# Two attention layers over 8 images: row 0 copied, bias rows, 264 columns, and other places for the steps of the sums

## Chip, cores and metric

The kernel runs on one core of a Trainium2 chip. The metric is the device time of one execution in microseconds (us), here the median of several runs; lower is better. An engine is written as in the profile: PE is TensorE's matmul, PEld its weight load, DVE VectorE, ACT ScalarE, POOL GpSimd, SP SyncE, which here only issues DMAs. "L857" is line 857 of the kernel before.

## What is computed

Eight images of 256 channels and 96x96 pixels in float32 go through two layers, each with a group norm ahead of it and the input added after it. Cut to what matters:

```python
# layer 0, on g = groupnorm(x)
q_f, k_f, v_f = (fft2(pconv(g, w, b), axes=(-2, -1)) for w, b in ((w1, b1), (w2, b2), (w3, b3)))
q_f, k_f = l2_normalize(q_f), l2_normalize(k_f)        # shape (b, 8 heads, 32, 9216)
attn = einsum('bhcn,bhdn->bhcd', q_f, k_f) * temperature
attn = complex(softmax(real(attn)), softmax(imag(attn)))
out = abs(ifft2(einsum('bhcd,bhdn->bhcn', attn, v_f), axes=(-2, -1)))   # over 32 and 9216
x = x + pconv(out, w_out)
# layer 1, on g = groupnorm(x)
q, k = softplus(Wq g + bq), softplus(Wk g + bk)        # 32 rows each
v = Wv g + bv
x = x + einsum(q, k v^T) / einsum(q, sum(k))
```

The forward transform is over the two axes of the image and the inverse one over the flattened 9216 pixels, so the two don't cancel: in the kernel each image row is turned by an amount that grows with the number of its row. Row 0 isn't turned at all.

## The kernel before

No transform is carried out. Layer 0's logits come from two 256x256 sums over pixels (`pair_sums`, L317), of the even part (x plus its mirror image) and of the odd part (x minus it). Everything is worked per image, and the stages of one image follow each other on PE: attention, woven into the turning of the rows (`attention` L364, `rotate` L524); `images` (L576, the 2-D maps, magnitude, output projection); `layer1` (L674); `output` (L829). Two arenas hold 256x9216 floats each and change roles from image to image: `x_of(b)` and `y_of(b)`.

**Weaving.** A stage is a generator that yields numbers. `weave` (L878) adds them up, and each time a whole one is due it takes one step of another generator. During attention the other is `rotate(b)`, one step for two rows. During images, layer1 and output the other is `pair_sums(b + 1)`, the sums of the next image: a step is four 128x128 transposes of 128 columns (tile `eoT`, L344), an ACT copy to `xT` (L347), and four products into the accumulators `acc` (L325), with its `bn_stats` on DVE (L259). The sums have 37 steps; those left over are taken in one go at the end (`finish`, L887). The last image has no next one. Whoever yields more in one place takes a step more there, and leaves one fewer for a later place. A part that is left under one at the end of a stage is dropped.

**Order.** In attention the order of PE is as written (L897), in output that of PE, DVE, POOL and SP (L903). Elsewhere a scheduler orders the instructions. PE, DVE, ACT, POOL and SP each run their own queue in order.

**Rotation.** `step` (L535) takes two rows at once: four transposes of 128x96 (`xr`, L546), an ACT copy (L557), and two steps later four products with a 96x97 window of the table `rt` (`y`, L549; each float32 product is two PE instructions, a transpose is one). DVE takes 96 of the 97 columns to `y_of(b)` as image column g, in reverse order (L554), and the last one to `ys` (L553). The window comes from DRAM by DMA (L531), its last column from `csn` on POOL (L532), which is zero for row 0.

**Attention.** `qkm` (L389) holds four rows of means of q and k; L394 adds the biases to them by four products of a column `b12col` with the identity; ACT copies them (L400). At the end L510 forms `mz` from the columns of `at`: 33 x 8 = 264 that are used and 24 that stay zero, which fill the 288 up to two blocks of 128 and one of 32; DVE scales them (L512).

**Denominators.** At the end of `layer1`, DVE copies `kx` (L796); PE transposes it (L799, L801); DVE makes `kse4` of it (L807); PE forms eight products `den` (L816) and two `am` (L822); DVE takes the reciprocal `rec` of `den` (L819). `output` spreads `rec` over the partitions by PE (L833) and multiplies `kq` by it on DVE (L838). The yields between are 0.5 (L797), 0.5 (L810), 1 (L825), and 1 after the first four normalizations (L850).

**Output.** For each of six `s` and two halves `m` there is a group of four products `o` of 32x128 by 32x384 (L857), one in each block of 32 rows of PE. Three of the four results are added to x by DVE (L862); the fourth is copied by ACT (L865) and added by POOL (L866). Each group ends with `yield 1` (L871). The transposes, `rec` and `o` all take their PSUM tiles from one pool of five (`psum`, L53), which are handed out in turn:

```python
    psum = ctx.enter_context(tc.tile_pool(name="psum", bufs=5, space=bass.MemoryType.PSUM))
                for j in range(NB):
                    ps = ps_tile(f"o_{b}_{s}_{m}_{j}")
```

**Start.** All 25 loads of image 0 stand first on SP. `tables` (L226) builds the lookup tables, among them `rt` by a DMA on SP (L249) that waits for DVE, and `load_small` (L198) puts 51 small loads behind it. It is called after the first step of the sums of image 0 (L892). The tables' inputs lie in the arena `y_of(0)` (L134).

Of the kernel before, what the change touches and what calls it, by code (L numbers as in the profile page):

```python
# [68 lines left out]
def two_layer_kernel(ctx: ExitStack, tc: tile.TileContext, x, w1t, b1, w2t, b2, w3, b3, wot, temp,  # L69
# [56 lines left out]
    def ps_tile(name):  # L126
        return psum.tile([P, 512], F32, tag="ps", name=name)

    def load_x(b, t):
        for c in (2 * (NT - 1 - t), 2 * (NT - 1 - t) + 1):  # L130
            for h, n in chunk_rows(c):
                nc.sync.dma_start(out=x_of(b)[:, :, x_col(h):x_col(h) + n * W], in_=x_v[b, :, :, h * W:(h + n) * W])
# [56 lines left out]
    wkq0 = const.tile([P, KC, 2, D], F32, name="wkq0")  # L189
    for c, v in enumerate((wkt, wqt)):  # L190
        nc.scalar.dma_start(out=wkq0[:, :, c, :], in_=v.rearrange("(k p) o -> p k o", p=P))
    b12col = const.tile([P, 4], F32, name="b12col")
    b3col = const.tile([P, KC], F32, name="b3col")
    bkq4 = const.tile([P, 2], F32, name="bkq4")
    tcol = const.tile([P, KC], F32, name="tcol")

    def load_small():
        for c, v in enumerate((b1, b2)):  # L198
            nc.sync.dma_start(out=b12col[:, KC * c:KC * c + KC], in_=v.rearrange("(k p) -> p k", p=P))
        nc.sync.dma_start(out=b3col, in_=b3.rearrange("(k p) -> p k", p=P))  # L200
        temp_f = temp.rearrange("h a b -> h (a b)")
        for h in range(C // HEAD):
            k, j = divmod(h, 4)
            nc.sync.dma_start(out=tcol[32 * j:32 * j + 32, k:k + 1], in_=temp_f[h].partition_broadcast(HEAD))
        for j in range(4):
            nc.sync.dma_start(out=bkq4[32 * j:32 * j + 32, 0:1], in_=bk.unsqueeze(1))
            nc.sync.dma_start(out=bkq4[32 * j:32 * j + 32, 1:2], in_=bq.unsqueeze(1))
        for j in range(16):
            for k in range(KC):
                c = (j, HEAD - j if j else 16)[k]  # L210
                nc.sync.dma_start(out=wo[NH * j:NH * j + NH, k, :], in_=wo_v[c])
# [78 lines left out]

    def even_odd(b, u):

        nr = PR if u < NT else 1
        t = ring_tile(f"eo_{b}_{u}").rearrange("p (c k n) -> p c k n", c=2, k=KC)
        x_t = image(x_of(b))
        rows = [PR * u + i for i in range(nr)]
        if u in (0, NT):
            parts = [(0, 1)] + ([(1, nr)] if nr > 1 else [])
        else:
            parts = [(0, nr)]  # L300
        for lo, hi in parts:
            n = hi - lo
            ra = x_col(rows[lo]) // W
            rp = x_col((H - rows[lo]) % H) // W
            back = slice(rp, rp - n if rp >= n else None, -1)
            for c in range(2):
                eng = nc.vector if u in (0, 1, NT) or (u == NT // 2 - 1 if b else u % 2) else nc.gpsimd
                op = (eng.tensor_add, eng.tensor_sub)[c]
                pop = (nc.gpsimd.tensor_add, nc.gpsimd.tensor_sub)[c]
                d = t[:, c, :, 0:nr * W].rearrange("p k (h w) -> p k h w", w=W)  # L310
                op(d[:, :, lo:hi, 1:W], x_t[:, :, ra:ra + n, 1:W], x_t[:, :, back, W - 1:0:-1])  # L311
                pop(d[:, :, lo:hi, 0:1], x_t[:, :, ra:ra + n, 0:1], x_t[:, :, back, 0:1])
        return t, nr * W
# [50 lines left out]
    def attention(b):  # L364
# [22 lines left out]
        for k in range(KC):  # L387
            for m in range(KC):
                nc.tensor.matmul(pb[32 * m:32 * m + 2, 0:2 * P], lhsT=dmm[:, k, :],  # L389
                                 rhs=w12[:, k, :].rearrange("p (c n) -> p c n", c=2)[:, :, m * P:(m + 1) * P],  # L390
                                 start=(k == 0), stop=False, skip_group_check=True)
        for c in range(2):
            for m in range(KC):
                nc.tensor.matmul(pb[32 * m:32 * m + 1, c * P:(c + 1) * P], lhsT=b12col[:, KC * c + m:KC * c + m + 1],  # L394
                                 rhs=ident, start=False, stop=(c == 1), skip_group_check=True)
        yield 1

        qkm = [scr[1][32 * m:32 * m + 2, 0:6 * P].rearrange("p (i c n) -> p i c n", i=3, c=2) for m in range(KC)]
        for m in range(KC):
            nc.scalar.copy(qkm[m][:, 0], pb[32 * m:32 * m + 2, 0:2 * P].rearrange("p (c n) -> p c n", c=2))  # L400
            nc.vector.tensor_scalar_mul(qkm[m][:, 1], qkm[m][:, 0], hw2[32 * m:32 * m + 2])
            nc.vector.tensor_mul(qkm[m][:, 2], qkm[m][:, 0], qkm[m][:, 1])
        pt = ps_tile(f"covT_{b}")
# [100 lines left out]

        MZ = (NZ + 3) * NH
        mz = one.tile([P, KC, MZ], F32, tag="wbig", name=f"mz_{b}")
        for k in range(KC):
            pm = ps_tile(f"mz_{b}_{k}")
            for m in range(KC):
                nc.tensor.matmul(pm[:, 0:MZ], lhsT=w3n[:, m, k * P:(k + 1) * P],  # L510
                                 rhs=at[:, m].rearrange("p n h -> p (n h)"), start=(m == 0), stop=(m == KC - 1))
            nc.vector.tensor_scalar_mul(mz[:, k, :], pm[:, 0:MZ], rstd[:, k:k + 1])  # L512
            yield 1

        m0[b] = mz, nmean, beta
# [8 lines left out]
    def rotate(b):  # L524

        y = image(y_of(b))
        ys = one.tile([P, KC, H + 1], F32, tag="ys", name=f"ys_{b}")

        def load_r(h):
            tm = three.tile([P, TR * (W + 1)], F32, tag="tm", name=f"tm_{b}_{h}")[0:W].rearrange("p (r w) -> p r w", r=TR)  # L530
            (nc.scalar if b else nc.sync).dma_start(out=tm[:, :, 0:W], in_=window(h))  # L531
            nc.gpsimd.tensor_copy(tm[:, :, W:W + 1], csn[0:W, 2, h:h + TR].unsqueeze(2))  # L532
            return tm

        def step(h, turned):  # L535

            if h is not None:
                pt = ps_tile(f"xr_{b}_{h}")
            if turned is not None:
                g, gt, tm = turned  # L540
                pu = ps_tile(f"y_{b}_{g}")
            for r in range(2):
                for k in range(KC):
                    if h is not None:
                        o = x_col(h + r)
                        nc.tensor.transpose(pt[0:W, r * C + k * P:r * C + (k + 1) * P], x_of(b)[:, k, o:o + W], ident)  # L546
                    if turned is not None:
                        o = (r * KC + k) * (W + 1)
                        nc.tensor.matmul(pu[:, o:o + W + 1], lhsT=gt[0:W, r, k * P:(k + 1) * P], rhs=tm[:, g % TR + r, :],  # L549
                                         start=True, stop=True)  # L550
            if turned is not None:
                src = pu[:, 0:2 * KC * (W + 1)].rearrange("p (r k w) -> p k w r", r=2, k=KC)
                nc.vector.tensor_copy(ys[:, :, g:g + 2], src[:, :, W, :])  # L553
                nc.vector.tensor_copy(y[:, :, :, g:g + 2], src[:, :, W - 1::-1, :])  # L554
            if h is not None:
                xt = xt_slot()
                nc.scalar.copy(xt[0:W, :, 0:C], pt[0:W, :].rearrange("p (r n) -> p r n", r=2))  # L557
                return xt

        tms = [load_r(g) for g in range(0, 3 * TR, TR)]  # L560
        pending = []
        for h in range(0, H, 2):
            if h % TR == 0:
                tm = tms.pop(0)
            if h % TR == 4 and 3 * TR <= h - 4 + 2 * TR < H:
                tms.append(load_r(h - 4 + 2 * TR))
            xt = step(h, pending.pop(0) if len(pending) == 2 else None)
            pending.append((h, xt, tm))
            yield
        for p in pending:  # L570
            step(None, p)
        y0[b] = ys
# [101 lines left out]
    def layer1(b):  # L674
# [119 lines left out]

        kxs = own[:, 0:C + 1]
        nc.vector.tensor_copy(kxs, kx[:, 0:C + 1])  # L796
        yield 0.5  # L797
        pt = ps_tile(f"kxT_{b}")
        nc.tensor.matmul(pt[:, C:C + 1], lhsT=rep4, rhs=kxs[:, C:C + 1], start=True, stop=True)  # L799
        for k in range(KC):  # L800
# [6 lines left out]
        nc.vector.tensor_scalar_mul(kse4, mask4, kse)  # L807
        kxT = own[:, 2 * C + 4:3 * C + 4].rearrange("p (k n) -> p k n", k=KC)
        nc.scalar.copy(kxT.rearrange("p k n -> p (k n)"), pt[:, 0:C])
        yield 0.5  # L810


        pd = ps_tile(f"den_{b}")
# [8 lines left out]
            nc.tensor.matmul(pa[:, 0:C], lhsT=kxT[:, k, :], rhs=wvs[:, k, :], start=(k == 0), stop=(k == KC - 1))  # L822
        am = own[:, 3 * C + 4:4 * C + 4]
        nc.vector.scalar_tensor_tensor(am, in0=bvs, scalar=ksum, in1=pa[:, 0:C], op0=ALU.mult, op1=ALU.add)
        yield 1  # L825

        l1[b] = x, kq, rec, am

    def output(b, x, kq, rec, am):  # L829
# [21 lines left out]
        for s in range(NS):  # L851
            for m in range(KC):
# [6 lines left out]
                for j in range(NB):  # L859
                    r = slice((NB * s + j) * CH, (NB * s + j + 1) * CH)  # L860
                    if j < NB - 1:
                        nc.vector.tensor_add(x[:, m, r], x[:, m, r], po[j][:, 0:CH])  # L862
                    else:
                        t = two.tile([P, CH], F32, tag="v16", name=f"po_{b}_{s}_{m}_{j}")
                        nc.scalar.copy(t, po[j][:, 0:CH])  # L865
                        nc.gpsimd.tensor_add(x[:, m, r], x[:, m, r], t)  # L866
                if alone and m == 0 and s + 1 < NS:
                    if s + 1 >= 4:
                        pds.append(select(s + 1, acc_tile(f"rec_{b}_{s + 1}")))
                    normalize(s + 1, pds[s + 1])  # L870
                yield 1  # L871
            if b + 1 < B and s in (1, NS - 1):
                load_x(b + 1, NT // 4 - 2 - s // 2 // 2)
            for j in range(NB):
# [14 lines left out]
            pass  # L889

    sums = pair_sums(0)
    next(sums)  # L892
    tables()
    finish(sums)
    turns = rotate(0)
# [62 lines left out]
```

## Time and profile before

| | us |
|---|---|
| median of 7 runs | 2776.03 (2774.57 to 2778.32) |
| the profiled execution | 2778.32 |
| its span, first to last instruction | 2776.2 |
| PE busy in it | 2728.7 (98%) |
| DVE, ACT, POOL busy | 1950.1, 1374.5, 835.2 |
| one image, from one `den` to the next | 341.2 |

The span is 2.1 us shorter than the profiled execution's own time; the rest lies around it. Most of the images take the same course: the first `den` product starts 341.2 us after that of the image before, for the images 1 to 6. In a timeline each line has the start, the time from the start of the first to the end of the last of its instructions, the engine and line, the operation, the tiles and the count; what the engine waited for stands in brackets. Matmuls are pipelined: the start of the next line tells more than the end of one.

### The profile page before, as it was taken

To read this page: it belongs to the slowest core of one execution; us is meant where nothing else is said; L and a number is where in the kernel's file an instruction comes from. 1 tells how busy PE (TensorE), PEld (TensorE's weight loads), DVE (VectorE), ACT (ScalarE), POOL (GpSimd) and SP (SyncE) were. 2 spreads that over 40 slices of the span, in tenths; PEclk is the share of its full clock that TensorE was granted. 3 is DMA by queue.
4 is the path that set the end of the run, shared out by engine and by line. 5 is a ranking of instruction groups with operands and counts; after the bars stand their busy time and mean duration, and the time that the engine had idled before them with its cause. 6 is when DMAs were issued, how large, how long until landed. Compare 5 with 4: busy or idle time off the path is not lost.

```text
span 2776.2 us, 47920 instructions
## 1 busy us (share of the span) xinstructions
PE 2728.7 (98%) x18460; PEld 1979.5 (71%) x18460; DVE 1950.1 (70%) x4088; ACT 1374.5 (50%) x2114; POOL 835.2 (30%) x914
## 2 busy tenths in 40 slices
PE   8999999999999999999999999999999999999988
PEld 8965679657795677956679566885678856788545
DVE  6577765876658766587675876758766687666766
ACT  3455634556345563355634546445554455544553
POOL 5033340343303424035140350413513134131311
PEclk9999999999999999999999999999999999999998
DMA  5120151201512015120151201521015210241003
GB/s 168 36 67 12 47 183 43 66 10 49 177 43 72 6 47 181 43 69 6 53 177 45 63 6 53 181 54 52 6 53 184 56 46 7 77 163 27 1 7 137
DMA packets 197810, 192.52 MB, mean 69 GB/s; under 512 B 89360, under 2 KB 197584, under 8 KB 197584
## 3 DMA queue, kind: packets, MB, share of 16 engines
q1 hardware_dynamic: 130336, 164.34, 18.6%
q10 hardware_dynamic: 67248, 25.12, 3.5%
q8 instruction: 147, 2.41, 0.4%
q14 instruction: 79, 0.65, 0.1%
HBM read 113.85 MB, written 75.57 MB: 68 GB/s over the span
## 4 chain that ended last, share of the span: by engine, by line
PE 94%; DVE 3%; ACT 2%; issue 0%; POOL 0%; DMA 0%; POOLq 0%; ACTq 0%; DVEq 0%
PE z L615 20%; PE po L627 18%; PE acc L325 13%; PE y L549 10%; PE xr L546 6%; PE eoT L344 5%; PE xT L773 5%; PE kq L712 5%; PE o L857 4%; PE kx L749 3%; PE cw L423 1%; DVE rec L819 1%; PE kT L764 1%; DVE arena L554 1%; PE mz L510 1%; PE cw L434 1%
## 5 line engine op out<-in xcount | busy, mean ns | idle before, releaser
L615 PE MATMUL z<-arena,mz 128*128 128x384 f32 (+2 forms) x2400 | 595.0, 476 | 0.0
L627 PE MATMUL po<-e,wo 128*128 128x384 f32 x1536 | 529.7, 486 | 0.2 <-ACT e L662 0.2
L661 POOL TENSOR_TENSOR e<-e 128x768 f32<-128x768 f32 x192 | 348.5, 1816 | 553.5 <-ACT e L660 553.5
L615 PEld LDWEIGHTS z<-arena,mz 128*128 128x128 f32 (+1 forms) x2400 | 325.6, 163 | 241.4 <-issue 42.4
L549 PE MATMUL y<-tm,xT 96*128 96x97 f32 x3072 | 477.6, 261 | 1.7 <-ACT sd_a L283 0.5
L549 PEld LDWEIGHTS y<-tm,xT 96*128 96x128 f32 x3072 | 462.6, 192 | 12.8 <-ACT xT L557 5.1
L325 PE MATMUL acc<-xT 128*128 128x256 f32 (+2 forms) x2368 | 440.2, 328 | 3.5 <-ACT xT L347 3.5
L627 PEld LDWEIGHTS po<-e,wo 128*128 128x128 f32 x1536 | 289.5, 190 | 197.7 <-DVE arena L629 1.2
L656 DVE TENSOR_TENSOR e<-z,xT 128x768 f32<-128x768 f32 x384 | 366.1, 953 | 88.2 <-PE z L615 88.2
L259 DVE BATCH_NORM_STATS2 st<-arena 128x6 f32<-128x384 f32 x768 | 406.5, 552 | 12.9 <-DMA arena<-in_x_dram 2.0
L546 PE MATMUL xr<-ident,arena 128*96 128x128 f32 x1536 | 413.6, 275 | 0.0
L325 PEld LDWEIGHTS acc<-xT 128*128 128x128 f32 (+1 forms) x2368 | 380.0, 191 | 37.6 <-ACT xT L347 5.2
L557 ACT COPY xT<-xr 96x512 f32<-96x512 f32 x384 | 222.2, 583 | 287.7 <-PE xr L546 286.1
L660 ACT ACTIVATE e<-e 128x1536 f32<-128x1536 f32 x192 | 284.6, 1482 | 92.5 <-DVE e L656 91.2
L662 ACT ACTIVATE e<-e 128x768 f32<-128x768 f32 x192 | 162.0, 844 | 334.4 <-POOL e L661 333.2
L311 POOL TENSOR_TENSOR eo<-arena 128x760 f32<-128x760 f32 x136 | 247.6, 1821 | 141.8 <-issue 133.2
L629 DVE TENSOR_TENSOR arena<-arena,po 128x384 f32<-128x384 f32 x384 | 211.3, 552 | 96.0 <-PE po L627 72.5
L347 ACT ACTIVATE xT<-eoT 128x512 f32<-128x512 f32 x280 | 166.8, 598 | 190.1 <-PE eoT L344 188.2
L532 POOL COPY tm<-csn 96x6 f32<-96x6 f32 x128 | 24.5, 192 | 753.8 <-PE y L549 550.7
L546 PEld LDWEIGHTS xr<-ident,arena 128*96 128x96 f32 x1536 | 230.1, 150 | 8.9 <-issue 5.6
L554 DVE COPY arena<-y 128x384 f32<-128x384 f32 x384 | 210.4, 548 | 0.8
L553 DVE COPY ys<-y 128x4 f32<-128x4 f32 x384 | 62.4, 163 | 207.1 <-PE y L549 205.1
(200 smaller groups left out, 3067.7 us busy)
## 6 DMA issues: line engine op xcount, KB each, us to landing
arena<-in_x_dram SPq DMA_DIRECT2D x184, 384.0 KB
out_dram<-arena SPq DMA_DIRECT2D x184, 384.0 KB
tm<-rt ACTq DMA_DIRECT2D x112, 216.0 KB
tm<-rt SPq DMA_DIRECT2D x16, 216.0 KB
arena<-in_x_dram SPq DMA_DIRECT2D x8, 288.0 KB
out_dram<-arena SPq DMA_DIRECT2D x8, 288.0 KB
wl<-in_w1t_dram SPq DMA_DIRECT2D x8, 256.0 KB
wl<-in_w2t_dram SPq DMA_DIRECT2D x8, 256.0 KB
```

The lines of the kernel that those rows point to most:

```text
L259: nc.vector.bn_stats(out=st[:, k, c, :], in_=x_of(b)[:, k, c * CH:(c + 1) * CH])
L311: op(d[:, :, lo:hi, 1:W], x_t[:, :, ra:ra + n, 1:W], x_t[:, :, back, W - 1:0:-1])
L325: mm = nc.tensor.matmul(acc[c][:, m * C:m * C + (KC - m) * P], lhsT=t[0:np_, c, m * P:(m + 1) * P], rhs=t[0:np_, c, m * P:C], start=(first ...
L546: nc.tensor.transpose(pt[0:W, r * C + k * P:r * C + (k + 1) * P], x_of(b)[:, k, o:o + W], ident)
L549: nc.tensor.matmul(pu[:, o:o + W + 1], lhsT=gt[0:W, r, k * P:(k + 1) * P], rhs=tm[:, g % TR + r, :], start=True, stop=True)
L554: nc.vector.tensor_copy(y[:, :, :, g:g + 2], src[:, :, W - 1::-1, :])
L557: nc.scalar.copy(xt[0:W, :, 0:C], pt[0:W, :].rearrange("p (r n) -> p r n", r=2))
L615: mm = nc.tensor.matmul(out[:, o:o + n * W], lhsT=columns(mz, k, c, j), rhs=y[:, k, h * W:(h + n) * W], start=(k == 0 and o == 0), stop=(k ...
L627: nc.tensor.matmul(po[:, 0:CH], lhsT=wo[:, k, m * P:(m + 1) * P], rhs=e[:, k, :], start=(k == 0), stop=(k == KC - 1))
L656: nc.vector.tensor_add(e[:, 2 * c:2 * c + 2, :].rearrange("p t (q h) -> p t q h", h=H), pz[:, 0:CH].rearrange("p (q h) -> p q h", h=H).uns ...
L660: nc.scalar.activation(e, e, AF.Square)
L661: nc.gpsimd.tensor_add(e[:, 0:2, :], e[:, 0:2, :], e[:, 2:4, :])
```

## The change

- `rotate`: row 0 is copied by POOL from x to column 0 of y, and its entry of `ys` is set to zero; its two transposes and two products, and its part of the copies L553, L554 and L557, are left out.
- biases: four rows are loaded by four DMAs in place of two column loads, the rest of a 64-partition block is cleared by POOL, and DVE adds them to `qkm` (two adds of 2x256) in place of the four products L394 and the two ACT copies L400.
- `mz`: the 24 zero columns are cleared by POOL ahead of time, and products and scaling go over 264 columns.
- yields: 1, 1 and 2 in place of 0.5, 0.5 and 1 at the denominators, and 1 and 2/3 in turn in place of 1 after the groups of the output, ahead of the last image's own normalizations rather than behind them.
- `tables`: called after twelve steps of the first image's sums and not after one.
- an assertion at build time, with a set `loaded`, which makes no instruction.

```diff
     def load_small():
+        nc.gpsimd.memset(b12[0:64], 0.0)
         for c, v in enumerate((b1, b2)):
-            nc.sync.dma_start(out=b12col[:, KC * c:KC * c + KC], in_=v.rearrange("(k p) -> p k", p=P))
+            for m in range(KC):
+                nc.sync.dma_start(out=b12[32 * m:32 * m + 1, c, :], in_=v[m * P:(m + 1) * P].unsqueeze(0))
...
-                                 start=(k == 0), stop=False, skip_group_check=True)
-        for c in range(2):
-            for m in range(KC):
-                nc.tensor.matmul(pb[32 * m:32 * m + 1, c * P:(c + 1) * P], lhsT=b12col[:, KC * c + m:KC * c + m + 1],
-                                 rhs=ident, start=False, stop=(c == 1), skip_group_check=True)
+                                 start=(k == 0), stop=(k == KC - 1), skip_group_check=True)
...
-            nc.scalar.copy(qkm[m][:, 0], pb[32 * m:32 * m + 2, 0:2 * P].rearrange("p (c n) -> p c n", c=2))
+            nc.vector.tensor_add(qkm[m][:, 0], b12[32 * m:32 * m + 2],
+                                 pb[32 * m:32 * m + 2, 0:2 * P].rearrange("p (c n) -> p c n", c=2))
...
+        nc.gpsimd.memset(mz[:, :, NZ * NH:MZ], 0.0)
...
-                nc.tensor.matmul(pm[:, 0:MZ], lhsT=w3n[:, m, k * P:(k + 1) * P],
-                                 rhs=at[:, m].rearrange("p n h -> p (n h)"), start=(m == 0), stop=(m == KC - 1))
-            nc.vector.tensor_scalar_mul(mz[:, k, :], pm[:, 0:MZ], rstd[:, k:k + 1])
+                nc.tensor.matmul(pm[:, 0:NZ * NH], lhsT=w3n[:, m, k * P:(k + 1) * P],
+                                 rhs=at[:, m, 0:NZ].rearrange("p n h -> p (n h)"), start=(m == 0), stop=(m == KC - 1))
+            nc.vector.tensor_scalar_mul(mz[:, k, 0:NZ * NH], pm[:, 0:NZ * NH], rstd[:, k:k + 1])
...
+        o = x_col(0)
+        nc.gpsimd.tensor_copy(y[:, :, :, 0], x_of(b)[:, :, o:o + W])
+        nc.gpsimd.memset(ys[:, :, 0:1], 0.0)
...
-                    if h is not None:
+                    if h is not None and h + r:
...
-                    if turned is not None:
+                    if turned is not None and g + r:
...
-                nc.vector.tensor_copy(ys[:, :, g:g + 2], src[:, :, W, :])
-                nc.vector.tensor_copy(y[:, :, :, g:g + 2], src[:, :, W - 1::-1, :])
+                r = 0 if g else 1
+                nc.vector.tensor_copy(ys[:, :, g + r:g + 2], src[:, :, W, r:2])
+                nc.vector.tensor_copy(y[:, :, :, g + r:g + 2], src[:, :, W - 1::-1, r:2])
...
-                nc.scalar.copy(xt[0:W, :, 0:C], pt[0:W, :].rearrange("p (r n) -> p r n", r=2))
+                r = 0 if h else 1
+                nc.scalar.copy(xt[0:W, r:2, 0:C], pt[0:W, r * C:2 * C].rearrange("p (r n) -> p r n", n=C))
...
         nc.vector.tensor_copy(kxs, kx[:, 0:C + 1])
-        yield 0.5
+        yield 1
...
         nc.scalar.copy(kxT.rearrange("p k n -> p (k n)"), pt[:, 0:C])
-        yield 0.5
+        yield 1
...
         nc.vector.scalar_tensor_tensor(am, in0=bvs, scalar=ksum, in1=pa[:, 0:C], op0=ALU.mult, op1=ALU.add)
-        yield 1
+        yield 2
...
+                yield (1, 2 / 3)[m]
                 if alone and m == 0 and s + 1 < NS:
...
                     normalize(s + 1, pds[s + 1])
-                yield 1
...
     sums = pair_sums(0)
-    next(sums)
+    for _ in range(NT):
+        next(sums)
     tables()
```

More of the change, by code (lines that the diff above doesn't have):

```diff
@@ L127, in ps_tile @@
         return psum.tile([P, 512], F32, tag="ps", name=name)
+    loaded = set()
     def load_x(b, t):
+        loaded.add((b, t))
         for c in (2 * (NT - 1 - t), 2 * (NT - 1 - t) + 1):
@@ L191, in two_layer_kernel @@
         nc.scalar.dma_start(out=wkq0[:, :, c, :], in_=v.rearrange("(k p) o -> p k o", p=P))
-    b12col = const.tile([P, 4], F32, name="b12col")
+    b12 = const.tile([P, 2, P], F32, name="b12")
     b3col = const.tile([P, KC], F32, name="b3col")
@@ L291, in even_odd @@
     def even_odd(b, u):
+        assert (b, u % NT) in loaded
         nr = PR if u < NT else 1
```

## Prediction

> **What bounds the kernel.** I read the busy shares and the chain first.
>
> ```profile
> PE 2728.7 (98%) x18460; PEld 1979.5 (71%) x18460; DVE 1950.1 (70%) x4088; ACT 1374.5 (50%) x2114; POOL 835.2 (30%) x914
> ...
> PE 94%; DVE 3%; ACT 2%; issue 0%; POOL 0%; DMA 0%; POOLq 0%; ACTq 0%; DVEq 0%
> ```
>
> PE is the bound nearly everywhere: 47.5 us of the span (2776.2 - 2728.7) are idle, 9.4 of them ahead of its first instruction. So PE work that goes is time that goes, but no step that only changes place on PE can win more than idle time. The list of PE's waits says how little there is at the denominators:
>
> ```profile
> PE rec L833 <- DVE rec L819: 5.2, 8, 1.6
> ...
> PE den L816 <- DVE own L807: 1.9, 8, 0.8
> ```
>
> The last image has 1.6 and 0.8 of that and no sums to fill it with; 3.6 and 1.1 remain for seven images, some 0.7 us each.
>
> **Work that goes (rotation and attention).** The timeline of PE in image 0:
>
> ```profile
> 80.14 0.27 PE L546 MATMUL xr<-ident,arena 128*96 128x128 f32 x1
> 80.25 0.36 PE L549 MATMUL y<-tm,xT 96*128 96x97 f32 x2
> 80.45 0.27 PE L546 MATMUL xr<-ident,arena 128*96 128x128 f32 x1
> ...
> 83.18 1.03 PE L389 MATMUL qkm<-wl,dmm 128*2 128x256 f32 x8
> 84.04 0.61 PE L394 MATMUL qkm<-ident,b12col 128*1 128x128 f32 x8
> 84.58 0.31 PE L546 MATMUL xr<-ident,arena 128*96 128x128 f32 x1
> ```
>
> From start to start a transpose and a product take 0.31 us, the transpose 0.11 of it. Row 0 loses two of each: 0.62 us per image, 8 x 0.62 = 5.0. The group norm's chain runs beside this: PE's second variance product L281 comes at 421.10 in image 1, ACT's square ends at 420.41, so L281 can come 0.62 earlier with 0.07 to spare, and what hangs on it moves along. If it didn't, the gain would be lost: between 0 and 5.0, I take 5.0, since the trace has the margin.
>
> L394 takes 84.58 - 84.04 = 0.54 us: 8 x 0.54 = 4.3. In its place DVE has two adds of 2x256; the nearest row, L402, is 0.41. DVE is busy 43.98 of the 75.15 us of the rotation, which hides them; without that cover they cost 8 x 0.82 = 6.6. ACT is relieved of L400.
>
> 24 columns fewer in four products: eight instructions of L325 with 768 columns together take 1.31 us, 1.7 ns a column, so 4 x 24 x 1.7 ns = 0.16 per image, 1.3 in all.
>
> At nothing: POOL's copy of row 0 and its memsets (POOL is busy 3.09 us of those 75.15; the copy stands behind the last `eo` and ahead of `tm_18`, and waits for the output DMAs of the image before, as DVE's first copy to y did already); the four loads in place of two, on an SP that idles; the shorter copies on ACT and DVE.
>
> **Tables later.** `pcs` (L239) no longer stands between the first transposes, where 10.83 to 11.56 are 0.73; later it costs some 0.3 (two one-column products, L799 has 0.15 for one): -0.4, between -0.73 and +0.3. The order of instructions puts the `rt` DMA behind DVE's table work, which comes after eleven `bn_stats` that follow `eo_5` (32.09 before): near 40 us in place of 24.29. Behind it on SP stand 45 small loads, 18.5 us by their rows (the 32 of `wo` 12.13), then the three `tm` loads: some 59 in place of 49.60. The first `y` needs them at 78.52, so nothing. POOL's copy of row 0 waits for `rt` too, with `eo_2` behind it, which PE wants at 56.6; if `rt` came 13 us later still, PE would wait.
>
> **The moved steps.** The totals of the yields give, per image but the last, four steps at the denominators where two were, and two fewer in the output. The order of the changed kernel shows where: a whole one ahead of `den`, two between `am` and `rec`; and the groups `o_0_1`, `o_1_0`, and `o_2_1`, `o_3_0`, stand side by side with no step between. What a step costs in the first place:
>
> ```profile
> 362.38 0.82 PE L325 MATMUL acc<-xT 128*128 128x256 f32 x4
> 363.35 1.50 PE L816 MATMUL den<-arena,own 128*32 128x384 f32 x16 [0.15 <-DVE own L807]
> 364.77 1.13 PE L822 MATMUL am<-wvs,own 128*128 128x256 f32 x4
> 365.74 0.60 PE L344 MATMUL eoT<-ident,eo 128*128 128x128 f32 x4
> 366.18 0.82 PE L325 MATMUL acc<-xT 128*128 128x256 f32 x4
> 367.51 0.93 PE L833 MATMUL rec<-rec,sel 32*128 32x384 f32 x8 [0.52 <-DVE rec L819]
> ```
>
> From `kxT` (361.70) to `rec` are 5.81 us, with work 0.68 + 0.66 + 1.42 + 0.97 + 0.44 + 0.66 = 4.83 and 0.98 without. Two more steps at 1.75 (a step's pace where nothing else runs) make 8.33; the reciprocal (2.56) then ends behind cover, and 0.24 stays for the changes of tile shape. So 8.57: +2.76 per image for 3.50 of work. What it saves in the output:
>
> ```profile
> 374.58 0.93 PE L857 MATMUL o<-arena,own 32*128 32x384 f32 x8
> ...
> 375.44 0.66 PE L344 MATMUL eoT<-ident,eo 128*128 128x128 f32 x4
> 375.53 1.48 DVE L862 TENSOR_TENSOR arena<-arena,o 128x384 f32<-128x384 f32 x3 [1.88 <-PE o L857]
> ...
> 377.33 0.93 PE L857 MATMUL o<-arena,own 32*128 32x384 f32 x8
> ```
>
> Four products run side by side in 0.86, all ready at the end; a step fills the time to the next group, 2.75 from group to group. Without the step the next group wants four of five PSUM tiles at once: one is free, the others come as DVE adds. In the last image, where no steps are:
>
> ```profile
> 2762.30 4.26 DVE L862 TENSOR_TENSOR arena<-arena,o 128x384 f32<-128x384 f32 x9
> ...
> 2763.83 0.30 PEld L857 LDWEIGHTS o<-arena,own 32*128 32x128 f32 x4 [0.17 <-DVE arena L862]
> 2764.30 0.29 PEld L857 LDWEIGHTS o<-arena,own 32*128 32x128 f32 x2 [0.17 <-DVE arena L862]
> ```
>
> Nine adds, one each 0.465, and PE waits for each. So behind the end of a group, with the adds 0.09 later: the third add frees its tile at 0.09 + 2 x 0.465 + 0.55 = 1.57, the last product starts at 1.63 and, if alone it takes as long as in four, ends at 2.49. With a step between it was 2.75. A removed step saves 0.26 (0.92, if a lone product takes a quarter of 0.86); two save 0.52. So a moved pair costs 2.76 - 0.52 = 2.24 us per image, between 0.92 and 2.98 (no idle filled); 7 x 2.2 = 15.4.
>
> A rule against this edit: the Trainium skill's page TensorEngine Tiling (Array Packing), section PSUM Bottleneck, says that splitting the array speeds up TensorE and not the emptying of PSUM, which may become the bottleneck. By it alone a bare group would take three adds, 1.40 us, a removed step would save 1.35, and the sum would be 2765.4. The rows say more: two groups between steps don't reach that pace, since PE stands behind the last tile.
>
> **Sum.** -5.0 - 4.3 - 1.3 - 0.4 + 15.4 = +4.4. The profiled execution, 2778.32, would become 2782.7; it was the slowest of seven, and from their median of 2776.03 I forecast **2780.4**. 0.2% (5.5 us) is about what a measurement of this kernel tells from no change, so this is just within.
>
> **Rivals.**
> - *The output hides the missing steps.* DVE idles 0.34 to 1.27 us per group there, and PE is called 98% busy. If each removed step saves its whole 1.89 (2.75 - 0.86), the moved pair gains 1.02, the sum is -11.0 - 7.1, 2758; at the pace of the adds alone 2765. Against it: five tiles, and the order of the changed kernel makes three of the second group's products wait for DVE. 0.20.
> - *POOL's queue, slower.* In the changed order the four instructions of `eo_4` (4.0 us) stand ahead of POOL's first add of the output, not behind it. ACT's copy in the second of two bare groups needs the buffer (`v16`, two) that this add gives back. By my times `eo_4` starts near 368 with its step and is done by 373. If it starts later than 376, ACT and then PE wait, 1 to 2 us per image: 7 to 14 us on top, 2787 to 2794. 0.12.
> - *The removed work was no bound, or the tables come late.* The 10.6 us lie beside DVE and ACT chains; if half of it is lost, 2785.7. Against: PE idles 0.92 of the 75.15 us. 0.06.
>
> **Numbers.** My case 0.62, its own range 2775 to 2786. Faster by over 0.2% (under 2770.5): the first rival and a little of mine, 0.22. Slower (over 2781.6): 0.25 of mine, and the two others, 0.41. Within: 0.37. The range leaves out the far half of the first rival and of the second: 2764 to 2788.
>
> **What the new profile would show.** `pcs` behind the twelfth step and no L394: right whatever the time. From `kxT` to `rec` 8.6 us. In the two bare groups PE's weight loads waiting for DVE's adds, and 3.35 from the first group's start to the next transposes, where the rows before have 0.86 + 2.75; if 1.8, the first rival holds. `rec` no longer waiting for L819 but in the last image. An `eo` transpose waiting for POOL, or ACT for POOL at `po_1_0`, is the second rival. Images 339 us apart (341.2 - 1.32 - 1.02) would mean that the moved steps are free; 342 or more are my case (341.2 - 1.32 + 2.2 = 342.1). A PE wait at the first `y` would show late tables.

## The result, and the profile after

The changed kernel takes **2783.63 us** (median of 14 runs, 2780.08 to 2785.44), the kernel before 2776.17 (34 runs). The ratio is 1.0025, with a 95% interval from 1.0018 to 1.0032: slower by 5 to 9 us. The forecast was 2780.4, in a range from 2764 to 2788.

The page of the changed kernel, busy shares and chain:

```profile
PE 2740.9 (99%) x18348; PEld 1987.0 (71%) x18348; DVE 1954.5 (70%) x4104; ACT 1365.8 (49%) x2098; POOL 844.3 (30%) x939
...
PE 95%; DVE 2%; ACT 2%; issue 0%; DMA 0%; POOL 0%; POOLq 0%; ACTq 0%; DVEq 0%
```

PE has 112 instructions fewer, yet 12.2 us more of busy time. Its idle time fell from 47.5 to 40.4 us (2781.3 - 2740.9). The waits that the moved steps were to fill are indeed gone; here are their lines in the list of PE's waits (us in total, times, longest):

```profile
PE rec L842 <- DVE rec L828: 1.6, 1, 1.6
...
PE den L825 <- DVE own L816: 0.8, 1, 0.8
```

Only the last image, which has no sums to fill with, still waits there; 3.6 and 1.1 us have gone from the other seven. So the idle time went down and the time went up: "busy" has grown somewhere without new work. PE's timeline at the denominators of image 0 (start, duration, engine and line):

```profile
360.96 0.69 PE L810 MATMUL kxT<-rep,own 128*128 128x128 f32 x4
361.49 0.60 PE L350 MATMUL eoT<-ident,eo 128*128 128x128 f32 x4
361.93 1.47 PE L331 MATMUL acc<-xT 128*128 128x256 f32 x8
363.33 1.50 PE L825 MATMUL den<-arena,own 128*32 128x384 f32 x16
364.75 1.13 PE L831 MATMUL am<-wvs,own 128*128 128x256 f32 x4
...
367.47 0.60 PE L350 MATMUL eoT<-ident,eo 128*128 128x128 f32 x4
367.91 1.47 PE L331 MATMUL acc<-xT 128*128 128x256 f32 x8
369.31 0.93 PE L842 MATMUL rec<-rec,sel 32*128 32x384 f32 x8
```

Three whole steps stand between `kxT` and `rec` (the middle one is left out here), and no line has a wait in brackets. From the first line of `kxT` (360.82) to `rec` are 8.49 us, 2.68 more than the 5.81 before; the 3.50 us of two steps came in, so 0.82 of idle time is filled. In the output, two groups stand side by side:

```profile
376.38 3.39 PE L866 MATMUL o<-arena,own 32*128 32x384 f32 x16
377.32 2.88 DVE L871 TENSOR_TENSOR arena<-arena,o 128x384 f32<-128x384 f32 x6 [0.94 <-PE o L866]
...
377.93 0.29 PEld L866 LDWEIGHTS o<-arena,own 32*128 32x128 f32 x2 [0.61 <-DVE arena L871]
...
378.39 0.29 PEld L866 LDWEIGHTS o<-arena,own 32*128 32x128 f32 x2 [0.17 <-DVE arena L871]
378.86 0.29 PEld L866 LDWEIGHTS o<-arena,own 32*128 32x128 f32 x2 [0.17 <-DVE arena L871]
...
379.70 0.66 PE L350 MATMUL eoT<-ident,eo 128*128 128x128 f32 x4
```

Read the first line with care: one row says that PE is "busy" for 3.39 us with 16 instructions, but the three weight loads below it show that three of the four products of the second group each wait for one of DVE's adds, 0.46 and 0.47 apart. A row of products that waits in the middle is counted as busy; that is where PE's 99% comes from. From 376.38 to the next transposes are 3.32 us, and so in all fourteen pairs of the trace; with a step between, the same two groups take 0.86 + 2.75 = 3.61. So a step of 1.75 us of work has gone and 0.29 us is won.

The measure used below is the distance of two images, from the first `z` product (L615 before, L624 after) of one to that of the next, the median of the seven in a trace. Most of them agree within 0.05 us in one trace (single ones are 0.1 to 1.4 longer), far finer than the times of whole executions, which spread over 6 us. The kernel before has 341.20, the changed one 342.08.

### The profile page after: what moved, and what is told of

It is laid out like the page before. It is cut to its first block, busy times and chain, and to the rows that moved or that the text cites. A ratio compares the mean times of both kernels' runs of the same rounds, so it can differ in the third digit from the quotient of the medians.

```text
span 2781.3 us, 47738 instructions
## 1 busy us (share of the span) xinstructions
PE 2740.9 (99%) x18348; PEld 1987.0 (71%) x18348; DVE 1954.5 (70%) x4104; ACT 1365.8 (49%) x2098; POOL 844.3 (30%) x939
## 4 chain that ended last, share of the span: by engine, by line
PE 95%; DVE 2%; ACT 2%; issue 0%; DMA 0%; POOL 0%; POOLq 0%; ACTq 0%; DVEq 0%
PE z L624 20%; PE po L636 18%; PE acc L331 13%; PE y L556 10%; PE xr L553 6%; PE eoT L350 5%; PE xT L782 5%; PE kq L721 5%; PE o L866 4%; PE kx L758 3%; PE cw L426 1%; PE kT L773 1%; DVE arena L562 1%; PE mz L514 1%; PE cw L437 1%; PE zs L595 0%
## 5 line engine op out<-in xcount | busy, mean ns | idle before, releaser
L624 PE MATMUL z<-arena,mz 128*128 128x384 f32 (+2 forms) x2400 | 594.9, 476 | 0.0
L624 PEld LDWEIGHTS z<-arena,mz 128*128 128x128 f32 (+1 forms) x2400 | 325.6, 163 | 241.4 <-issue 42.4
L553 PE MATMUL xr<-ident,arena 128*96 128x128 f32 x1520 | 409.2, 275 | 0.0
L566 ACT COPY xT<-xr 96x512 f32<-96x512 f32 (+1 forms) x384 | 220.5, 579 | 293.8 <-PE xr L553 287.5
L553 PEld LDWEIGHTS xr<-ident,arena 128*96 128x96 f32 x1520 | 227.2, 150 | 10.3 <-issue 6.9
L562 DVE COPY arena<-y 128x384 f32<-128x384 f32 (+1 forms) x384 | 209.9, 547 | 1.2 <-issue 0.5
L561 DVE COPY ys<-y 128x4 f32<-128x4 f32 (+1 forms) x384 | 62.4, 162 | 199.4 <-PE y L556 197.0
```

The lines of the kernel that those rows point to most:

```text
L562: nc.vector.tensor_copy(y[:, :, :, g + r:g + 2], src[:, :, W - 1::-1, r:2])
L566: nc.scalar.copy(xt[0:W, r:2, 0:C], pt[0:W, r * C:2 * C].rearrange("p (r n) -> p r n", n=C))
L624: mm = nc.tensor.matmul(out[:, o:o + n * W], lhsT=columns(mz, k, c, j), rhs=y[:, k, h * W:(h + n) * W], start=(k == 0 and o == 0), stop=(k ...
```

## Experiments

### The moved steps undone, the moved steps alone, the removed work alone

`moves_undone` is the changed kernel with the yields of before:

```diff
         nc.vector.tensor_copy(kxs, kx[:, 0:C + 1])
-        yield 1
+        yield 0.5
...
         nc.scalar.copy(kxT.rearrange("p k n -> p (k n)"), pt[:, 0:C])
-        yield 1
+        yield 0.5
...
-        yield 2
+        yield 1
...
-                yield (1, 2 / 3)[m]
+                yield 1
```

> The changed kernel with the four yields as before (half a step, half a step and one at the denominators, one behind every group of the output); row 0, the biases, the 24 columns and the later tables stay changed. Theory (the moved steps cost 2.1 us per image but the last, by the two traces 2.68 lost between kxT and rec and 0.57 won in the output): images 340.0 us apart, 14.8 us less than the changed kernel, so 2768 to 2770 us, 0.2 to 0.3% under the kernel before. Rival A (the moved steps cost nothing, and the time went up because the removed work was no bound, the tables come late or POOL's new copy holds PE up): 2782 to 2785 us as the changed kernel. Rival B (part of the rise is the half granted clock in the last image's output, whatever the steps): 2768 plus up to 3 us.

`moves_alone` is the kernel before with the same edit the other way round.

> The kernel before with nothing changed but the yields: one, one and two at the denominators, 1 and 2/3 in the output. Theory: 7 x 2.1 = 14.8 us more, 2791 us, images 343.3 us apart (341.2 + 2.1), kxT to rec 8.4 where 5.8 was, 3.3 from the first of two bare groups to the next transposes. Rival A (the moved steps are free): 2776 us, images 341.2 apart.

`work_gone` is `moves_undone` with the tables in their old place as well:

```diff
-    for _ in range(NT):
-        next(sums)
+    next(sums)
     tables()
```

> The kernel before with row 0 copied, the biases as rows and the 24 columns left out, but yields and tables as before. Theory: by the forecast's terms -5.0 - 4.3 - 1.3 = -10.6, by the rotations of the two traces 8 x -1.2 = -9.6: 2765.6 to 2766.6 us; tables in their old place are worth 0.3 to 0.7 us against the kernel with the moves undone. Rival A (this work was no bound): within 2 us of 2776. Against the kernel with the moves undone this one tells what the later tables cost: by the forecast they save 0.4, by the trace of the changed kernel they cost some 0.3 to 0.7.

| kernel | images apart | median us | ratio to before, 95% interval |
|---|---|---|---|
| `moves_undone` | 339.97 | 2768.54 | 0.9972, 0.9961 to 0.9982 |
| `moves_alone` | 343.30 | 2792.88 | 1.0060, 1.0048 to 1.0073 |
| `work_gone` | 339.97 | 2767.54 | 0.9968, 0.9957 to 0.9979 |

The moved steps cost 343.30 - 341.20 = 2.10 us per image on the kernel before, and 342.08 - 339.97 = 2.11 on the kernel without the removed work: the two parts of the change don't touch each other. Over seven images that is 14.7 us. It is what the two places give: 2.68 more at the denominators, less 2 x 0.29 won in the output. Rival A falls: the moved steps aren't free, and the removed work was on the bound, 1.23 us per image.

### The two kernels once more

`before_again` and `after_again` are the kernel before and the changed one, unchanged, for a second trace of each.

> The kernel before, unchanged, for a second trace of it. Theory: 2776 us, no difference; images again 341.2 us apart to 0.1. The first profiled execution took 2778.3, 2.1 over the median of the runs: if the images are 341.2 apart in both, that lies ahead of the first image's products or in the last image's output, where the granted clock is at half in places, and the two traces will differ there and nowhere else. Rival B expects a last image (from its kxT to its last o) that differs by 1 to 3 us between the two.

> The changed kernel, unchanged, for a second trace and more times. By the distances of images (7 x 0.88 more, 1.23 less in image 0) it should stand 4.9 us over the kernel before; the medians differ by 7.5. Rival B (the rest is where half-clock stretches fall in the last image): images again 342.08 apart, and the time moves by the 2 us by which a last image with two stretches of 6.8 us at half clock is longer than one with two of 3.4: some executions near 2781, others near 2784. If all executions lie above 2783, that account is wrong or the place of the stretches is fixed by the kernel.

`before_again` took 2776.19 us (ratio 0.9999, 0.9990 to 1.0008), with images 341.18 apart; `after_again` 2783.64 (1.0024, 1.0015 to 1.0033), with images 342.08 apart. What differs between the two traces of the kernel before is the last image: from its first `z` product to the end of the span 233.8 us in the first and 231.3 in the second. Two stretches of it run at half the granted clock. Here they are, in the first trace and then in the second (the columns are the stretch, its sum and the busy time of each engine with its instructions, then PE's clock, the DMA share and GB/s):

```profile
2680.20:2687.00 6.80, 6.29 (x66) 2.76 (x70) 1.79 (x7) 1.18 (x2) 0.00 (x0) 0.50 0.02 4
2687.00:2704.00 17.00, 14.34 (x169) 6.50 (x159) 9.53 (x18) 14.58 (x27) 0.00 (x0) 1.00 0.00 1
2704.00:2710.90 6.90, 5.96 (x28) 5.63 (x28) 5.22 (x11) 3.56 (x7) 0.00 (x0) 0.51 0.00 0
```

```profile
2681.30:2684.80 3.50, 3.50 (x49) 1.48 (x42) 0.51 (x3) 0.00 (x0) 0.00 (x0) 0.51 0.03 7
...
2705.20:2708.60 3.40, 3.40 (x18) 3.16 (x16) 3.15 (x7) 2.27 (x4) 0.00 (x0) 0.51 0.00 0
```

Both come with a wait of PE that only the last image has (2.73 us for the group norm's statistics, 3.6 for the softplus ahead of `kT`). In the first trace each lasts 6.8 us, in the second 3.4, and the last image is 2.5 us longer in the first. All of that is ahead of its `kxT` (194.45 and 191.84 us from its first `z` product), not behind it, where the expectation had put it: from `kxT` to the last `o` product the second trace is the longer one (31.81, the first 29.25), which does not reach the end, as the last section shows.

The other traces agree. Seven have two stretches of 6.8 us, and their last images take 233.4 to 234.3 us; five have two of 3.4 us, and 231.3 to 232.5 us. Both traces of the changed kernel (233.8 and 233.6) and `moves_alone` are of the long kind, `moves_undone` and `work_gone` (231.8 both) of the short one; `sixth_no_moves` and `act_and_sixth`, further down, have only one such stretch. The length goes with the place of the drop. Where the clock drops at most 1.60 us after the end of the 2.73 us wait (eight traces), the first stretch is long, and PE idles another 0.55 us or more in the 3.4 us behind the drop. Where it drops 1.73 to 2.53 us after that end (six traces), the stretch is short, and PE idles 0.42 us or less there.

That bears on how the forecast was counted. The profiled execution of before (2778.32) was one with the long stretches, and most of its executions are shorter: of the 97 timed in all, 63 lie below 2777. Of 24 of the changed kernel four lie between 2780.1 and 2780.9, one at 2782.3 and 19 between 2783.1 and 2785.4, which is what the expectation of Rival B gave as a mixture of two kinds. Compared long with long, the two first profiled executions differ by 2783.19 - 2778.32 = 4.87 us, where the sum of the forecast was 4.4. Part of this closeness is luck: both profiled executions of the changed kernel have long stretches, and they are 1.8 us apart (2783.19 and 2784.98), 1.2 of it ahead of the first `z` product.

The mean granted clock, measured for 63 executions of the kernel before and 25 of the changed one, points the same way. It is 0.992 in the six traces with two long stretches and half clock in all of the last output, and 0.993 in the five with two short ones. 19 of the 25 have 0.992, and 8 of the 63. It doesn't settle single executions (two of the four near 2781 have 0.992 too). Why the changed kernel falls on the long stretches more often is open.

### Why a bare group is slow: the order in which tiles come back

`act_first` changes which of a group's four products ACT (with POOL) takes, and nothing on PE:

```diff
-                    if j < NB - 1:
+                    if j != (NB - 1 if alone else 0):
```

> The changed kernel, in which ACT (with POOL) takes the first of the four products of each output group, not the last, in all images but the last; DVE takes the other three. Nothing else moves on PE. Theory (the second of two bare groups waits for tiles in the order in which they were given out, and ACT's early copy comes back last in that order, unused): its last product then waits for DVE's second add of the first group, not the third, 0.465 us earlier. From the first bare group's start to the next transposes 3.31 becomes 2.85, the images 342.08 - 2 x 0.465 = 341.15 us apart, 6.5 us less in all: 2777 us. Rival C (the bare groups are slow for another reason, the products' own time or POOL's adds): 3.3 and 342.1 as before, 2783 us, or slower if POOL's buffers hold ACT up.

`sixth_moves` gives one product of every first group of a slice the PSUM tile that `kx` had:

```diff
-                    ps = ps_tile(f"o_{b}_{s}_{m}_{j}")
+                    ps = (acc_tile if j == 1 and m == 0 and not alone else ps_tile)(f"o_{b}_{s}_{m}_{j}")
```

> The changed kernel, in which the second product of every first output group of a slice (the second of two bare ones) takes a sixth PSUM tile, the one that kx had, idle in this stage. Theory: two tiles are free at the start of that group and only two of DVE's adds have to come: 0.465 us earlier, 3.31 becomes 2.85, images 341.15 us apart, 2777 us. Rival C: 342.1 apart and 2783 us. If both this and the kernel with ACT first gain the same, the tiles are shown as the cause from two sides.

`act_first` has images 341.12 apart (341.15 expected) and takes 2775.12 us (ratio 0.9997, 0.9987 to 1.0006): 0.96 of the moved steps' 2.11 us per image is won back with no edit of PE's work. PE's weight loads in its second bare group:

```profile
378.43 0.41 PEld L866 LDWEIGHTS o<-arena,own 32*128 32x128 f32 x4 [0.54 <-ACT po L874]
379.01 0.29 PEld L866 LDWEIGHTS o<-arena,own 32*128 32x128 f32 x2 [0.17 <-DVE arena L871]
379.85 0.42 PEld L350 LDWEIGHTS eoT<-ident,eo 128*128 128x128 f32 x4 [0.55 <-POOL arena L875]
```

Two waits where three were, the first of them for ACT; the pair starts at 376.96, so 2.90 to the next transposes in place of 3.32. Rival C falls. That the distance agrees to 0.03 with the expected one is partly luck: the two pairs give 2 x 0.42 = 0.84 where 0.93 was expected, and the last group of the output, which no theory had, gives 0.13 (from its start to the next transposes 1.15 became 1.02).

`sixth_moves` has 2.85 there (374.95 to 377.80), as expected, but images 340.33 apart where 341.15 were: 0.82 better than the theory. It takes 2770.04 us (0.9973, 0.9964 to 0.9983). The rest is in the first group of the output, which no theory had. The kernel with the removed work alone shows it, without any bare group:

```profile
370.46 0.58 PE L866 MATMUL o<-arena,own 32*128 32x384 f32 x1
...
371.84 0.29 PEld L866 LDWEIGHTS o<-arena,own 32*128 32x128 f32 x2 [0.63 <-DVE arena L847]
...
372.68 0.42 PEld L350 LDWEIGHTS eoT<-ident,eo 128*128 128x128 f32 x4 [0.55 <-issue]
```

The selected reciprocals `rec_4` and `rec_5` hold two of the five tiles until DVE has multiplied by them (L847), so this group waits too: 2.22 us from 370.46 to the next transposes. The kernel before has it too (its first group starts at 370.47 and the next at 374.58, here 370.46 and 374.57), inside a row of "busy" PE.

### The sixth tile without the moved steps, and both remedies with them

`sixth_no_moves` is `work_gone` with the sixth tile; `act_and_sixth` is the changed kernel with both edits.

> Row 0 copied, biases as rows, 24 columns left out, tables and yields as in the kernel before, and the second product of each first output group of a slice in the sixth PSUM tile, the one that kx had. Theory (in the kernel with the sixth tile and the moved steps 0.9 of the 1.76 won per image lay in the two bare groups and 0.83 in the first group, whose products wait for tiles that the selected reciprocals hold until DVE has multiplied): without bare groups only the 0.83 is left, images 339.97 - 0.83 = 339.14 us apart, 5.8 us under the kernel with the removed work alone: 2762 us, the fastest so far, and the moved steps still cost 340.32 - 339.14 = 1.2 per image with that tile. Rival D (the tile is worth 1.76 wherever the steps lie, so that the steps are not what it helps): 338.2, 2755 us.

> The changed kernel with both: ACT takes the first product of a group, and the second product of each first group has the sixth tile. Theory: in the second bare group two tiles are free and the other two come back at the same time, from ACT's copy and DVE's first add, so 3.31 becomes 2.40 and the images are 340.32 - 0.92 = 339.4 apart, 2764 us; a moved pair then costs 2.68 - 2 x (3.61 - 2.40) = 0.26 per image over the kernel with the sixth tile and no moves: close to nothing, but no gain. If the pace of DVE's adds were still the bound: 340.3 as with the sixth tile alone.

`sixth_no_moves` has images 339.20 apart and takes **2761.06 us** (0.9946, 0.9933 to 0.9958), faster than both kernels. Its first group:

```profile
369.50 0.59 PE L866 MATMUL o<-arena,own 32*128 32x384 f32 x2
...
369.92 0.94 PE L866 MATMUL o<-arena,own 32*128 32x384 f32 x6
370.97 0.63 PE L350 MATMUL eoT<-ident,eo 128*128 128x128 f32 x4
```

1.47 us in place of 2.22. Rival D falls: without the moved steps the tile is worth 0.77, with them 1.75; of the 0.98 between, 2 x 0.46 lies in the bare pairs (3.32 became 2.86).

`act_and_sixth` takes 2764.65 us (0.9957, 0.9942 to 0.9973). Its bare pair takes 2.44 (375.72 to 378.16, 2.40 expected), but its images are 339.89 apart, not 339.4. The missing 0.5 lies behind the last group of the output, where in six of the seven images PE's transposes wait for POOL's `eo` (the even and odd parts for the sums of the next image) a second time, and POOL had waited for the load of the next image:

```profile
1767.52 1.75 POOL L318 TENSOR_TENSOR eo<-arena 128x6 f32<-128x6 f32 x4 [0.16 <-DMA arena<-in_x_dram]
...
1769.05 0.41 PE L350 MATMUL eoT<-ident,eo 128*128 128x128 f32 x2 [0.25 <-POOL eo L318]
```

The transpose before this one starts 0.53 us earlier, where 0.11 is usual: 0.42 lost. The one image without this second wait has the distance 339.42, which is 0.22 over the 339.20 of `sixth_no_moves`, where the expectation had 0.26. So with the bare groups freed this far, a moved pair costs 339.89 - 339.20 = 0.7 us per image, some 0.2 of it as expected and the rest at this wait.

### The removed work part by part

`row0_alone`, `biases_alone` and `mz_alone` are the kernel before with only the edits to the rotation, to `qkm` with its loads, and to `mz`. There is one execution of each, read by the distance of its images.

> The kernel before, in which only row 0 is copied and not rotated. The measure is the distance of the images in the trace, which agrees to some 0.03 us within a kernel. Forecast: 341.19 - 0.62 = 340.57. Rival A (the group norm's chain on DVE and ACT is the bound there): 341.2. All removed work together gave 1.23 where 1.32 was forecast; theory: the 0.09 is lost in this part, since ACT's square root now ends later against PE, so 340.66.

> The kernel before, in which only the biases of q and k are rows, added by DVE, and the eight products with the identity are gone. Forecast: images 341.19 - 0.54 = 340.65 us apart. Rival A (DVE's two new adds are not hidden, 0.82): 341.5. If the missing 0.09 is here, 340.74.

> The kernel before, in which only the 24 columns of zeros are left out of the four products and set by POOL. Forecast: images 341.19 - 0.16 = 341.03 us apart. By difference of the kernel with all removed work and those with row 0 and the biases alone (1.22 - 0.62 - 0.42): 341.01.

Row 0 gives 340.57 (0.63 less; forecast 0.62), the biases 340.77 (0.43; forecast 0.54), the columns 341.04 (0.16; forecast 0.16). The three make 1.22, all of the 1.23. The theory that the missing 0.1 lay in row 0 is wrong; it is in the biases. PE's timeline of the changed kernel in image 1:

```profile
424.45 1.03 PE L395 MATMUL qkm<-wl,dmm 128*2 128x256 f32 x8
425.41 0.31 PE L553 MATMUL xr<-ident,arena 128*96 128x128 f32 x1
```

The eight products of two columns now take 0.96 us to the next row's start; with L394 behind them it was 0.86 (83.18 to 84.04). In both kernels all eight products stand on few columns (128*2, and 128*1 in L394) and a full transpose comes last, so before, the 0.10 was paid behind L394: 0.86 + 0.54 = 1.40 in all, now 0.96, which is 0.44 less. The Trainium skill's page TensorEngine Tiling (Array Packing), section Key Properties, has a rule that fits, that a change of the tiling mode drains TensorE. Whether the 0.10 is such a drain or the load of the next weights, these rows don't separate.

## Where the prediction was right, and where not

- **What bounds the kernel.** Right: PE's work that goes is time that goes, 1.23 of 1.32 us per image. But the 47.5 us of idle time aren't all that can be won without less work: the sixth tile won 0.77 us per image inside a row called busy.
- **Row 0, the columns.** Right: 0.63 and 0.16 for 0.62 and 0.16. That the group norm's chain moves along held.
- **Biases.** The term was mis-sized: 0.43 per image and not 0.54. L394's 0.54 was read from its start to the start of the next row, which takes in 0.10 for what comes behind products of few columns; that stays when L394 goes. DVE's two adds are hidden, as the forecast had it.
- **Tables later.** `pcs` runs behind the twelfth step, `rt` was issued at 41.55 (near 40 forecast), the `tm` loads until 62.94 (some 59), and PE doesn't wait at the first `y`. The price of -0.4 isn't shown, nor refuted: from the first transposes to the first `xr` the six traces with late tables have 67.4 to 69.4 us (mean 68.5) and the eight with early ones 67.8 to 69.2 (mean 68.4), and two traces of one kernel differ by 0.6 and 0.9. A part of this scatter is at the first products: the first eight `acc` take 2.56 from start to start in the changed kernel (11.39 to 13.95) and in `work_gone` (13.00 to 15.56), 2.12 in before (12.69 to 14.81), and 1.31 later.
- **The moved steps.** Right in mechanism and nearly in size: 8.49 from `kxT` to `rec` for 8.57, 3.32 for a bare pair for 3.35, 2.10 per image for 2.24, 14.7 us in all for 15.4 (which is 7 x 2.2; with 2.24 it is 15.7). The images of the changed kernel are 342.08 apart; 342.1 was forecast.
- **Rivals.** The first, that the output hides the missing steps, fell with the three weight loads and with `moves_alone`; no bare pair reached its 1.8, even with a sixth tile and ACT in front (2.44). The price by the pace of DVE's adds alone fell with it: how many tiles are free and in which order they return decides. The Trainium skill's page TensorEngine Tiling (Array Packing), section PSUM Bottleneck, names the right resource; these rows show that its pace alone doesn't give the time. The second, POOL's queue, didn't come: PE waits for POOL's `eo` 1.3 us in seven times, as before. Its `eo_4` had more room than forecast: the four instructions ahead of POOL's first add of the output (375.14) start at 353.60, not near 368, and are done by 357.51. A second wait for `eo` in an image came only with ACT in front (two images of `act_first`, six of `act_and_sixth`). The third fell with `work_gone`.
- **The sum.** By the distances it is 7 x 0.88 - 1.2 (image 0, whose rotation only loses) = +5.0; the forecast had +4.4, with the moved steps 0.7 us too dear, which nearly made up for the biases, 0.9 us too good, and with the tables' -0.4, which no trace shows. The medians differ by 7.46, and the measured one lies 3.2 us above the forecast. What failed is the last step, from the profiled execution to the median: the forecast took the sum over to the median of the seven runs as if they were of one kind, but the profiled one had long half-clock stretches in its last image, and most of the others have times that fit short ones. Against 2778.32 the forecast's own 2782.7 is 0.5 from the profiled 2783.19. That most runs of the changed kernel have the long stretches fits their times, their mean clocks and both traces, but isn't shown for each run.

## What to carry to other kernels

Before work is moved from one place to fill a short wait in another, ask what it covers where it stands: these steps filled 0.82 us of idle time at the denominators and left the output without the time in which its PSUM tiles came back, for 2.1 us per image. A row of matmuls that is called busy can hide waits; look at its weight loads, and at the order in which the tiles were given out, since a tile that is back early is of no use if it is last in that order. And where images repeat, their distance in one trace tells parts of 0.1 us that the medians of whole runs can't.

## What the runs showed of the hardware

- The granted clock drops to half for 3.4 or 6.8 us at single waits of PE of 2.7 and 3.6 us near the end of the run, and the edges in one trace (2680.2, 2687.0, 2704.0, 2710.9) are 2, 5 and 2 times some 3.4 us apart. Whether half clock lasts one such window or two differs between two runs of the same kernel, whose last images are 2.5 us apart. The wait of 2.73 us (with 0.26 and 0.93 us of idle time close behind) brought half clock in all fourteen traces, the one of 3.6 us in twelve. The Trainium skill's page TensorE: Matmul & The Clock Gate, section The HAM clock gate, gives a window of 3413 ns that runs freely, which agrees with these edges. It asks for a whole idle window before the clock drops, while in the 3.4 us ahead of these drops PE was idle for only 1.8 to 2.7 us.
- In the last image's output PE runs at half clock for some 30 us, and it costs next to nothing there: from the first store's issue to the end of the span are 28.35 us in the trace of before, where 10 us of this stretch ran at full clock, and 28.41 in `before_again`, where all of it was at half. The stores move 351 GB/s in that stretch of the changed kernel, at a DMA share of 0.98, and set the end.
- In attention, eight products on two columns take 0.86 us to the next start when products on one column follow, and 0.96 when a full transpose does. A price read from one start to the next takes in what follows.
